# A three-layer graph network on one core: node blocks and places in the prologue, own rows and own products at other points in layers 1 and 2

## The chip, the core and the metric

The kernel runs on one core of a Trainium2 chip. A core has a matrix engine (PE, TensorE), a vector engine (DVE), a scalar engine with an activation table (ACT), a general engine (POOL, GpSimd) and an engine that here does nothing but start DMA transfers (SP, SyncE). Each engine takes its own instructions in the order in which they stand in the program, and waits at an instruction until what it needs is there. DMA transfers run beside the engines; they too are started in the order of the queue that they stand in. The metric is the time of one launch in microseconds of the device, the median of several runs.

## The reference

There are 6250 nodes with 256 features each and 100000 edges (src to dst), sorted by dst. Two GATv2 attention layers (4 heads of 64, with a loop edge at each node), the input added and normalized, then one GAT layer (8 heads of 32), added and normalized again:

```python
def _gatv2_layer(x, src, dst, n, Wl, Wr, att, b):
    xl = (x @ Wl).reshape(n, H, C)
    xr = (x @ Wr).reshape(n, H, C)
    e = jax.nn.leaky_relu(xl[src] + xr[dst], NEG_SLOPE)
    logits = jnp.einsum('ehc,hc->eh', e, att)
    m = jax.ops.segment_max(logits, dst, num_segments=n)
    ex = jnp.exp(logits - m[dst])
    denom = jax.ops.segment_sum(ex, dst, num_segments=n)
    alpha = ex / (denom[dst] + 1e-16)
    msg = xl[src] * alpha[:, :, None]
    out = jax.ops.segment_sum(msg, dst, num_segments=n)
    return out.reshape(n, H * C) + b
...
    h = _gatv2_layer(x, src, dst, n, Wl1, Wr1, att1, b1)
    h = jax.nn.elu(h)
    h = _gatv2_layer(h, src, dst, n, Wl2, Wr2, att2, b2)
...
x = _layernorm(x + _L0_gnn_ref(...), axis=-1)
x = _layernorm(x + _L1_gnn_ref(x, W, a, src, dst), axis=-1)
```

In the third layer Wh = x W per head, the logit of an edge is leaky_relu(s1[src] + s2[dst]) with s1 and s2 two projections of Wh, and the output is the softmax-weighted sum of Wh[src].

## The kernel before

**Blocks by degree.** The nodes are sorted by falling number of incoming edges into 49 blocks of 128, one node to a partition. Block b has a fixed number of neighbour slots, cols[b], from 27 in block 0 down to 9 in block 48. A row of a table for one slot of 128 nodes is fetched by one indirect DMA that POOL issues (`gather_rows`, L1300). In layers 1 and 2 there is one slot more, slot 0, for the node's own row (the loop edge).

**Prologue** (`make_plan`). From dst it finds each node's edges: the ends of the runs in 128 pieces of 784 edges by max and match_replace, eight at a time, 64 at most (L953, L955); counts by one-hot products (L981 to L986); the beginning of each list (begin_i), on which POOL fetches the pieces of the lists (piece_of, L1016, 17 gathers); each node's place in the order of degrees (place_f, place); then from to_hi, given and to_lo (L1088) the inverse, node_i, by 49 products on PE. moved (L1113 to L1123) and fill (L1133, L1140) bring the lists into their final form, and POOL stores them in near_d (L1143, six stores). `wrong`, `bad` and `fits` check that the plan holds; otherwise a general path is taken.

In between, table 1 is made: xl1 = x Wl1 with four more columns, 260 in all, in 49 blocks of 128 consecutive nodes. `load_x` loads x in seven parts of seven blocks on SP, `keep_x` stores the parts beside the lists in near_d, `turn` transposes a block (PE, then ACT's copy), `table` multiplies it and stores its 130 KB on SP (L860). `tables(n)` does n blocks; the calls are spread by hand over the prologue, in the order in which engines are to take them: 12, 1, 1, 1, 1, 12, 8, 4, and 9 more. The last column of table 1, a node's place, is written by a DMA of its own on ACT's queue, one number to a row (L1064). Two loads of W and a of layer 3 and the biases stand at the end of SP's prologue.

**Layers 1 and 2** (`layer2(0, ...)` and `layer2(1, ...)`). One loop over the 49 blocks, with the order of the instructions written out by hand. The iteration of block b issues, in this order: the loads of block b+3 (`start`), the gathers of block b+1 (`gather`), what block b+1 needs of its own (`ready`, which calls `own`: xr in PSUM, named pr, and a function that puts the own row into slot 0 of the first gathered tile), then `attend(b)`: DVE's max (z, L1571 or L1591), product (L1594) and sum (L1595) per tile of up to nine slots, the copy of the own row of b+1, the softmax weights (ACT exponentials, L1446), the first z of block b+1 (`first_z`, L1571), then `finish(b-1)`, the shares (L1451, L1452), ACT's copy by of some weights (L1473), the weighting (DVE at L1483, ACT at L1482), the sum over slots on PE (acc, L1490), and last the part of `finish(b-1)` that makes the rows of the next layer and stores them.

In layer 1, `own1` transposes the block's x (L1420, L1422) and multiplies it by Wl (pl) and Wr (pr); pl is copied into slot 0 by ACT (L1684). `finish1` makes two rows of layer 2's tables (pm, ACT L1704), stored by SP (L1708, L1709). In layer 2, `start2` loads the own rows of both tables into `two` three blocks ahead (SP, L1717, L1718); `own2` has ACT copy one half to pr (L1724) and the other into slot 0 (L1725). `finish2` normalizes, makes the row of layer 3's table (ACT L1738) and stores it (SP, L1740).

**Between layers.** `follow` stands in the iteration of block 47: the first 14, 12 and 11 gathers of the next layer's blocks 0, 1 and 2 (`EARLY`) read only rows of blocks 0 to 44 (`LATE = 4`), the lists having been sorted for that; the others read all rows. The gathered tiles are a ring of nine (`rowp`). Layer 3 has the same blocks without slot 0 and is summed on DVE.

Of the kernel before, what the change touches and what calls it, by code (L numbers as in the profile page):

```python
# [714 lines left out]
def make_plan(  # L715
# [39 lines left out]
    rowp = ctx.enter_context(tc.tile_pool(name="table1_row", bufs=10))  # L755
# [62 lines left out]
    def rows(i):  # L818
        return min(P, N - i * P)

    xs, turned, at = {}, {}, [0]

    def blocks(j):
        return j * PART, min((j + 1) * PART, N // P)

    def load_x(j):
        b0, b1 = blocks(j)
        xs[j] = work.tile([P, PART, F], F32, name="xt")
        nc.sync.dma_start(
            xs[j][:, : b1 - b0, :], x[b0 * P : b1 * P, :].rearrange("(c p) f -> p c f", p=P)  # L830
        )

    def keep_x(j):
        b0, b1 = blocks(j)
        nc.sync.dma_start(
            near_d[b0 * P : b1 * P, CM:].rearrange("(c p) f -> p c f", p=P), xs[j][:, : b1 - b0, :]
        )

    def turn(i):
        j, k = divmod(i, PART)  # L840
        if k == 0 and 2 <= j + 2 < NB // PART:
            load_x(j + 2)
        if k == 2:
            keep_x(j)
        xt = xs[j][:, k, :] if rows(i) == P else x_end
        pt = pst.tile([P, 2, P], F32, name="pt")
        for c in range(2):
            nc.tensor.transpose(pt[:, c, :], xt[:, c * P : (c + 1) * P], ident)
        turned[i] = work.tile([P, 2, P], F32, name="xT")
        nc.scalar.copy(turned[i], pt)  # L850

    def table(i):
        xT = turned.pop(i)
        w = wc[0].rearrange("p j c h d -> p j c (h d)")
        pm = pst.tile([P, W2], F32, name="pm")
        for c in range(2):
            nc.tensor.matmul(pm, xT[:, c, :], w[:, 0, c, :], start=c == 0, stop=c == 1)
        xl = rowp.tile([P, W2], F32, name="xl")
        nc.scalar.copy(xl, pm)
        nc.sync.dma_start(xl1_d[i * P : (i + 1) * P, :W2], xl)  # L860
# [24 lines left out]
    if rest:  # L885
# [19 lines left out]
    x_end = filled_tile("x_end", [P, F], 0.0)  # L905
# [13 lines left out]
    each_hi = iota("each_hi", [P, NB, NB], [[0, NB], [1, NB]], dtype=BF16)  # L919
    each_lo = iota("each_lo", [P, NB, P], [[0, NB], [1, P]], dtype=BF16)  # L920
    vals = one.tile([P, 3, NB], BF16, name="vals")
    nc.gpsimd.iota(vals[:, 0, :], pattern=[[0, NB]], base=0, channel_multiplier=1,
                   allow_small_or_imprecise_dtypes=True)
    nc.gpsimd.iota(vals[:, 1, :], pattern=[[1, NB]], base=0, channel_multiplier=0,
# [12 lines left out]
    edge = one.tile([P, RUNS + 1], F32, name="edge")  # L937
    nc.vector.memset(edge[:, :1], float(KE))
# [6 lines left out]
    )  # L945
    runs = one.tile([P, KE], F32, name="runs")
# [5 lines left out]
    for r in range(0, RUNS, 8):  # L952
        nc.vector.max(ends[:, r : r + 8], runs)  # L953
        if r + 8 < RUNS:
            nc.vector.match_replace(runs, ends[:, r : r + 8], runs, 0.0)  # L955
    tables(12)
    load(0, "r")
    for what in "lar":
        load(1, what)
    run_i = one.tile([P, RUNS], I32, name="run_i")  # L960
# [11 lines left out]
    nc.vector.tensor_copy(edge[:, 1:], part[:, 2, :])  # L972
    size = one.tile([P, RUNS], BF16, name="size")
    nc.vector.tensor_sub(size, edge[:, :RUNS], edge[:, 1:])
# [83 lines left out]
    nc.vector.tensor_scalar(vals[:, 2, :], count, 255.0, None, op0=OP.min)  # L1058
# [4 lines left out]
    with nc.allow_non_contiguous_dma(reason="one number to a row"):  # L1063
        nc.scalar.dma_start(  # L1064
            xl1_d[:NP, W2:].rearrange("(p b) w -> p b w", b=NB), place_f.unsqueeze(2)
        )
    nc.sync.dma_start(x_end[: rows(NB - 1)], x[(NB - 1) * P :, :])
    nc.sync.dma_start(near_d[(NB - 1) * P :, CM:], x_end)
# [5 lines left out]

    tables(12)


    to_hi = one.tile([P, NB, NB], BF16, name="to_hi")
    nc.vector.tensor_tensor(
        to_hi, each_hi, to[:, 1, :].unsqueeze(2).to_broadcast([P, NB, NB]), op=OP.is_equal  # L1080
    )
    given = one.tile([P, NB, 3, NB], BF16, name="given")
    for j in range(3):
        nc.vector.tensor_mul(
            given[:, :, j, :], to_hi, vals[:, j, :].unsqueeze(2).to_broadcast([P, NB, NB])
        )
    to_lo = one.tile([P, NB, P], BF16, name="to_lo")
    nc.vector.tensor_tensor(  # L1088
        to_lo, each_lo, to[:, 0, :].unsqueeze(2).to_broadcast([P, NB, P]), op=OP.is_equal
    )  # L1090
    pp = ps.tile([P, 3, NB], F32, name="pp")
    for b in range(NB):
        nc.tensor.matmul(pp, to_lo[:, b, :], given[:, b], start=b == 0, stop=b == NB - 1)
    tables(8)
# [12 lines left out]

    moved = one.tile([P, SEGS, STEP, WIDE], I32, name="moved")
# [39 lines left out]
    for k in spans:  # L1148
        lacking(*k)
        fill(*k)  # L1150
    tables(4)
    got = one.tile([P, 3, NB], F32, name="got")
    nc.vector.tensor_copy(got, pp)
    nc.vector.scalar_tensor_tensor(
        node_i, got[:, 0, :], float(NB), got[:, 1, :], op0=OP.mult, op1=OP.add
    )

    wrong = one.tile([P, KE + 2 * NB + 1], F32, name="wrong")  # L1160
    nc.vector.tensor_tensor(wrong[:, : KE - 1], dst_e[:, : KE - 1], dst_e[:, 1:], op=OP.is_gt)
    nc.vector.tensor_tensor(wrong[:, KE - 1 : KE], dst_e[:, KE - 1 :], next_e, op=OP.is_gt)
    nc.vector.tensor_tensor(wrong[:, KE : KE + NB], got[:, 2, :], most, op=OP.is_gt)
    nc.vector.tensor_tensor(
        wrong[:, KE + NB : KE + 2 * NB], off.rearrange("p s j -> p (s j)")[:, :NB],
        off_i.rearrange("p s j -> p (s j)")[:, :NB], op=OP.not_equal,
    )
    nc.vector.tensor_mul(
        wrong[:, KE + NB : KE + 2 * NB], wrong[:, KE + NB : KE + 2 * NB], count
    )  # L1170
    nc.vector.tensor_scalar(
        wrong[:, KE + 2 * NB :], base[:, :1], float(E), None, op0=OP.not_equal
    )
    bad = one.tile([P, 2], F32, name="bad")
    nc.vector.reduce_sum(bad[:, :1], wrong, axis=AX.X)
    nc.vector.tensor_scalar(
        bad[:, 1:], got[:, 2, :1], -float(held), 0.0, op0=OP.add, op1=OP.max
    )
    tables(NB)
    pb = ps.tile([P, 2], F32, name="pb", tag="ph")  # L1180
    nc.tensor.matmul(pb, ones, bad, start=True, stop=True)
    right(0)
    left(1, nc.vector)
    right(1)
    many = one.tile([P, 1], F32, name="many")
    nc.vector.tensor_scalar(many, pb[:, 1:], float(P), None, op0=OP.is_gt)
    nc.vector.tensor_add(many, many, pb[:, :1])
    nc.vector.tensor_scalar(fits, many, 0.0, None, op0=OP.is_equal)
    for c in range(2):
        nc.sync.dma_start(  # L1190
            wh[:, c, :F].rearrange("p (h d) -> p h d", h=H1),
            w3[:, c * P : (c + 1) * P, :].rearrange("h p d -> p h d"),
        )
    tables(7)
    for k, b in enumerate(biases):
        nc.sync.dma_start(
            fixed[:, k, :], bass.AP(tensor=b.tensor, offset=b.offset, ap=[[0, P], [1, F]])
        )
    for k, h in enumerate((a3[:, :D1], a3[:, D1:])):
        nc.sync.dma_start(  # L1200
            fixed[:, 2 + k, :].rearrange("p (h d) -> p h d", h=H1),
            bass.AP(tensor=h.tensor, offset=h.offset, ap=[[0, P], [2 * D1, H1], [1, D1]]),
        )
# [4 lines left out]
def tile_by_degree(  # L1208
# [62 lines left out]
    nc.sync.dma_start(wh_d[NP:], nobody[:, 1, :A1])  # L1271

# [263 lines left out]
    def layer2(i, table, of, width, start, own, finish, follow):  # L1536
# [5 lines left out]
        with ExitStack() as es:  # L1542
# [19 lines left out]
            def ready(b):  # L1562
                pr, put = own(work, ps, pst, b, state[b][0][0][:, 0, :W2])
                state[b].append(pr)
                later.append(put)
# [58 lines left out]
            for b in range(3):  # L1624
                if (i, b) not in loaded:
# [3 lines left out]
            gather(0)  # L1629
            ready(0)  # L1630
            later.pop()()
# [3 lines left out]
            for b in range(NB):  # L1635
# [27 lines left out]
                if b == 0:  # L1663
                    nc.tensor.matmul(acc, edges_of, few, start=False, stop=True)
                if last:
# [11 lines left out]

    def own1(work, ps, pst, b, row):
        xT = transposed(work, pst, x1[:, b, :])
        pl = pst.tile([P, W2], F32, name="pl", tag="tp")  # L1680
        product(pl, xT, wc[0][:, 0])
        pr = ps.tile([P, W2], F32, name="pr")
        product(pr, xT, wc[0][:, 1])
# [31 lines left out]
    def start2(b):  # L1715
        two = twop.tile([P, 2, W2], F32, name="two")
        nc.sync.dma_start(two[:, 0, :], xl2_d[b * P : (b + 1) * P])  # L1717
        nc.sync.dma_start(two[:, 1, :], xr2_d[b * P : (b + 1) * P])  # L1718
        kept[b] = two

    def own2(work, ps, pst, b, row):
        two = kept.pop(b)
        pr = ps.tile([P, W2], F32, name="pr")
        nc.scalar.copy(pr, two[:, 1, :])  # L1724
        return pr, lambda: nc.scalar.copy(row, two[:, 0, :])  # L1725
# [20 lines left out]
    kept, loaded = {}, set()  # L1746

    def begin2():
        begin(1, xl2_d, W2)
        for b in range(3):  # L1750
            start2(b)
            loaded.add((1, b))

    layer2(0, xl1_d[:, :], sources, W2 + 1, start1, own1, finish1, begin2)
# [118 lines left out]
```

## Time and profile before

| what | value |
|---|---|
| median of 3 runs | 3332.04 us (3331.96 to 3335.03) |
| the profiled execution's own time | 3328.12 us |
| its span | 3326.3 us |
| granted TensorE clock, mean | 0.711 |
| DVE, POOL, PE, ACT busy, share of the span | 83%, 73%, 43%, 33% |
| bytes moved by DMA | 395.84 MB, 119 GB/s |
| first gather of layer 1, of layer 2, of layer 3 | 131.25, 1211.98, 2235.97 us |

A group of the page gives line, engine, operation, written and read tiles and the count; then busy time and the mean of one in ns; then the idle time of the engine just before, and what ended most of it. In the timeline each line has start, length, engine, line, operation, and in brackets how long the engine stood before it and who released it; SPq is SP's queue, and "issue" is time for which the profile shows no wait. A stretch gives for each engine busy time and count, then the granted clock, the DMA engines' mean busy share and GB/s.

### The profile page before, as it was taken

Reading aid. Unit: us, or ns where it says so; the run is one execution under the profiler, and the core shown is the slowest. Engines: PE = TensorE matmul, PEld = TensorE weight load, DVE = VectorE, ACT = ScalarE, POOL = GpSimd, SP = SyncE. Lnnn points to the kernel's source line nnn. Section 1 sums busy time; section 2 is a strip of 40 time slices with the busy share of each in tenths; the row PEclk is TensorE's granted clock in tenths of the full one; section 3 lists DMA queues with packets and bytes.
Section 4 is the critical chain, followed back from the end, with each engine's and each line's share of the span. In section 5 each row is a group of like instructions: output and inputs, shape, how many; then the busy total and the mean of one; then the engine's idle time right before and its main releaser. Section 6 shows DMA issues by size and latency. Waiting matters only on the chain.

```text
span 3326.3 us, 24261 instructions
## 1 busy us (share of the span) xinstructions
PE 1416.2 (43%) x5423; PEld 1131.0 (34%) x5424; DVE 2755.3 (83%) x2527; ACT 1108.0 (33%) x4428; POOL 2435.2 (73%) x2588
## 2 busy tenths in 40 slices
PE   7346666666677773565656666662000000000000
PEld 5235554555555552454545454552000000000000
DVE  7599998889888888999999999985966767666766
ACT  3134434444444442444445666561000000000000
POOL 5477777777777767777777777767777777777776
PEclk8678888888888886777877878886555555555555
DMA  8744444444444444444444444444333333333333
GB/s 198 145 111 118 117 118 121 118 120 122 121 121 121 124 111 112 122 121 127 121 127 126 132 126 132 131 111 115 108 107 107 108 108 107 108 107 107 107 107 86
DMA packets 189103, 395.84 MB, mean 119 GB/s; under 512 B 56249, under 2 KB 107963, under 8 KB 188934
## 3 DMA queue, kind: packets, MB, share of 16 engines
q0 software_dynamic: 121392, 339.19, 39.0%
q1 hardware_dynamic: 59858, 53.27, 5.7%
q10 hardware_dynamic: 7700, 1.74, 0.5%
q8 instruction: 47, 0.77, 0.1%
q14 instruction: 106, 0.87, 0.1%
HBM read 354.02 MB, written 40.42 MB: 119 GB/s over the span
## 4 chain that ended last, share of the span: by engine, by line
POOL 23%; DVE 15%; issue 13%; PE 7%; DMA 3%; ACT 1%; DVEq 0%; POOLq 0%; ACTq 0%
POOL g L1300 22%; PE acc L1490 6%; DVE g L1483 3%; DVE z L1594 3%; DVE lg L1595 3%; DVE z L1571 3%; DVE z L1591 2%; DMA g<-xl_d,near_r 1%; POOL out L1812 1%; DMA out<-y,node_i 1%; PE pm L1427 1%; DVE stats L1522 0%; DMA g<-whs_d,near_r 0%; ACT sd L1526 0%; DVE weighted L1503 0%
## 5 line engine op out<-in xcount | busy, mean ns | idle before, releaser
L1300 POOL DMA_INDIRECT g<-xl_d,near_r x1569 | 1484.4, 946 | 485.8 <-issue 434.8
L1490 PE MATMUL acc<-g,ident 128*128 128x256 f32 x3408 | 972.0, 455 | 654.2 <-DVE g L1483 357.6
L1490 PEld LDWEIGHTS acc<-g,ident 128*128 128x128 f32 x3408 | 788.8, 235 | 838.3 <-DVE g L1483 378.4
L1300 POOL DMA_INDIRECT g<-whs_d,near_r x766 | 727.1, 949 | 233.3 <-issue 227.2
L1482 ACT ACTIVATE g<-g,by 128x64 f32<-128x64 f32 x2308 | 561.0, 336 | 1.6
L1595 DVE TENSOR_REDUCE lg<-z 128x28 f32<-128x1820 f32 (+4 forms) x234 | 497.4, 2125 | 8.1
L1594 DVE TENSOR_TENSOR z<-z,at 128x1820 f32<-128x1820 f32 (+4 forms) x234 | 496.9, 2124 | 4.7
L1483 DVE TENSOR_TENSOR g<-g,wt 128x1792 f32<-128x1792 f32 (+8 forms) x234 | 331.8, 1435 | 31.9 <-ACT by L1473 31.9
L1512 DVE TENSOR_REDUCE acc_v<-weighted 128x256 f32<-128x4096 f32 (+15 forms) x49 | 343.7, 7014 | 1.6
L1591 DVE TENSOR_TENSOR z<-g,pr 128x1820 f32<-128x1820 f32 (+3 forms) x138 | 299.6, 2171 | 23.2 <-DMA g<-xl_d,near_r 14.8
L1456 ACT ACTIVATE wt<-lg 128x128 f32<-128x128 f32 (+17 forms) x49 | 14.0, 285 | 803.6 <-DVE lg L1455 803.6
L1782 DVE TENSOR_TENSOR lg<-g,s_r 128x56 f32<-128x56 f32 (+4 forms) x111 | 22.4, 214 | 268.5 <-DMA g<-whs_d,near_r 212.2
L1571 DVE TENSOR_TENSOR z<-g,pr 128x2080 f32<-128x2080 f32 (+4 forms) x96 | 197.9, 2061 | 44.5 <-DMA g<-xl_d,near_r 13.5
L1503 DVE TENSOR_TENSOR weighted<-g,wt 128x1792 f32<-128x1792 f32 (+4 forms) x111 | 226.6, 2057 | 0.1
L1422 ACT COPY xT<-pt 128x256 f32<-128x256 f32 x147 | 55.0, 374 | 505.8 <-PE pt L1420 505.8
L1446 ACT ACTIVATE wt<-lg,top 128x19 f32<-128x19 f32 (+14 forms) x392 | 115.7, 295 | 234.2 <-DVE top L1439 224.7
L1427 PE MATMUL pm<-wcat,xT 128*128 128x260 f32 x392 | 99.0, 395 | 22.6 <-ACT xT L1422 22.6
L1427 PEld LDWEIGHTS pm<-wcat,xT 128*128 128x128 f32 x392 | 70.4, 189 | 42.8 <-ACT xT L1422 34.3
L1446 ACT ACTIVATION_READ_ACCUMULATOR wt<-lg,top 128x1 f32 x392 | 73.5, 187 | 0.0
L1812 POOL DMA_INDIRECT out<-y,node_i x49 | 50.1, 1022 | 25.8 <-issue 14.2
L1427 PE MATMUL pm<-wh_cat,xT 128*128 128x272 f32 x196 | 59.0, 424 | 22.6 <-ACT xT L1422 22.6
L1427 PE MATMUL pl<-wcat,xT 128*128 128x260 f32 x196 | 57.2, 415 | 25.2 <-ACT xT L1422 25.2
(250 smaller groups left out, 1527.3 us busy)
## 6 DMA issues: line engine op xcount, KB each, us to landing
g<-xl_d,near_r POOLq DMA_INDIRECT x1569, 2.8
g<-whs_d,near_r POOLq DMA_INDIRECT x766, 2.8
whs_d<-row SPq DMA_DIRECT2D x49, 132.0 KB, 2.0
xl_d<-xl SPq DMA_DIRECT2D x49, 130.0 KB, 7.9
xl_d<-row SPq DMA_DIRECT2D x49, 130.0 KB, 2.6
xr_d<-row SPq DMA_DIRECT2D x49, 130.0 KB, 2.9
two<-xl_d SPq DMA_DIRECT2D x49, 130.0 KB, 2.9
two<-xr_d SPq DMA_DIRECT2D x49, 130.0 KB, 3.3
```

The source lines that it names most:

```text
L1300: nc.gpsimd.indirect_dma_start(out=g[:, j + own - s0, :width], out_offset=None, in_=table, in_offset=source(of, b, j),)
L1427: nc.tensor.matmul(pm, xT[:, c, :], w[:, c, :], start=c == 0, stop=c == 1)
L1446: nc.scalar.activation(wt[:, :, h], lg[:, :S, h], AF.Exp, bias=top[:, h : h + 1], accum_out=den[:, h : h + 1],)
L1482: nc.scalar.mul(g4[:, t, h, :], g4[:, t, h, :], by[:, t - m, h : h + 1])
L1483: nc.vector.tensor_mul(g4[:, :m], g4[:, :m], wt[:, s0 : s0 + m, :].unsqueeze(3).to_broadcast([P, m, H, F // H]),)
L1490: nc.tensor.matmul(acc, ident, g4[:, t], start=False, stop=s0 + t == S - 1 and not more)
L1503: nc.vector.tensor_mul(prod[:, s0 - base : s1 - base, :].rearrange("p t (h d) -> p t h d", h=H), g[:, :n, :F].rearrange("p t (h d) -> p t ...
L1512: nc.vector.reduce_sum(part, prod[:, : s1 - base, :].rearrange("p s f -> p f s"), axis=AX.X)
L1571: nc.vector.tensor_max(z, rows[0][:, :n, :W2], xr[:, None, :].to_broadcast([P, n, W2]))
L1591: nc.vector.tensor_max(z, g[:, :n, :W2], xr[:, None, :].to_broadcast([P, n, W2]))
L1594: nc.vector.tensor_mul(z, z, at[:, None, :].to_broadcast([P, n, W2]))
L1595: nc.vector.reduce_sum(lg[:, s0:s1, :], z.rearrange("p t (h d) -> p t h d", h=H2), axis=AX.X)
```

## The change

It has four parts.

In the **prologue**, a block of table 1 is no longer 128 consecutive nodes but the nodes p·49 + b, p being the partition, which is how places and counts are laid out. x comes in parts of seven such blocks (one run of 7168 bytes per partition), and table 1 goes out seven blocks at a time with the place as its last column (`put_rows`), once the places are known; the DMA of single numbers is gone. The last partitions hold no node in some blocks: POOL zeroes them in the four last parts before they are loaded.

The run ends are found in two halves of each piece, 32 each. The inverse of the places is made from one-hots in groups of 16 blocks. The check and the node numbers stand ahead of moved and fill. The biases are loaded on ACT's queue, W and a of layer 3 by SP after the prologue. The calls of tables are 9, 1, 1, 1, 1, 1, 1, 1, 8 and 25.

In **layer 1**, x's transposition and the product pr of block b+2 are issued in the iteration of block b, after the sum and before the rows of `finish1`; `own1` has only pl left.

In **layer 2**, `two` holds only the row of xr. The own row is loaded by SP directly into slot 0, from `own2`, and ACT's copy is gone.

```diff
-    rowp = ctx.enter_context(tc.tile_pool(name="table1_row", bufs=10))
+    rowp = ctx.enter_context(tc.tile_pool(name="table1_row", bufs=4))
...
     def load_x(j):
-        b0, b1 = blocks(j)
+        b0, b1 = j * PART, (j + 1) * PART
         xs[j] = work.tile([P, PART, F], F32, name="xt")
-        nc.sync.dma_start(
-            xs[j][:, : b1 - b0, :], x[b0 * P : b1 * P, :].rearrange("(c p) f -> p c f", p=P)
-        )
+        if b1 <= odd:
+            nc.sync.dma_start(
+                xs[j],
+                bass.AP(tensor=x.tensor, offset=x.offset + b0 * F,
+                        ap=[[NB * F, P], [F, PART], [1, F]]),
+            )
+            return
+        k = max(odd - b0, 0)
+        nc.gpsimd.memset(xs[j][P - 32 :, k:, :], 0.0)
+        for p0, p1 in ((0, whole // 16 * 16), (whole // 16 * 16, whole)):
+            nc.sync.dma_start(
+                xs[j][p0:p1],
+                x[p0 * NB : p1 * NB, :].rearrange("(p b) f -> p b f", b=NB)[:, b0:b1, :],
+            )
...
+    def put_rows(j):
+        b0, b1 = j * PART, (j + 1) * PART
+        rows = made.pop(j)
+        nc.scalar.copy(rows[:, :, W2], placed[0][:, b0:b1])
+        nc.sync.dma_start(of_nodes(xl1_d[:NP], b0, b1), rows)
+
     def table(i):
...
-        xl = rowp.tile([P, W2], F32, name="xl")
-        nc.scalar.copy(xl, pm)
-        nc.sync.dma_start(xl1_d[i * P : (i + 1) * P, :W2], xl)
+        if k == 0:
+            made[j] = rowp.tile([P, PART, W2 + 1], F32, name="xl")
+        nc.scalar.copy(made[j][:, k, :W2], pm)
+        if k + 1 == PART and placed:
+            put_rows(j)
...
-    for r in range(0, RUNS, 8):
-        nc.vector.max(ends[:, r : r + 8], runs)
-        if r + 8 < RUNS:
-            nc.vector.match_replace(runs, ends[:, r : r + 8], runs, 0.0)
-    tables(12)
+    for h, part_runs in enumerate((runs[:, HALF:], runs[:, :HALF])):
+        for r in range(h * HR, (h + 1) * HR, 8):
+            nc.vector.max(ends[:, r : r + 8], part_runs)
+            if r + 8 < (h + 1) * HR:
+                nc.vector.match_replace(part_runs, ends[:, r : r + 8], part_runs, 0.0)
+    tables(9)
...
-    with nc.allow_non_contiguous_dma(reason="one number to a row"):
-        nc.scalar.dma_start(
-            xl1_d[:NP, W2:].rearrange("(p b) w -> p b w", b=NB), place_f.unsqueeze(2)
-        )
...
+    placed.append(place_f)
+    for j in sorted(made):
+        if (j + 1) * PART <= at[0]:
+            put_rows(j)
...
+    for b0 in range(0, NB, T):
+        n = min(T, NB - b0)
+        s = slice(b0, b0 + n)
+        oh_hi = hot.tile([P, NB, T], BF16, name="oh_hi")[:, :, :n]
...
+        if b0 + n < NB:
+            tables(1)
...
-    tables(NB)
+    tables(8)
...
-    def layer2(i, table, of, width, start, own, finish, follow):
+    def layer2(i, table, of, width, start, ahead, own, finish, follow):
...
+            for b in range(2):
+                ahead(work, ps, pst, b)
             ready(0)
...
+                if b + 2 < NB:
+                    ahead(work, ps, pst, b + 2)
                 if last:
                     last[0]()
...
+    def ahead1(work, ps, pst, b):
+        xT = transposed(work, pst, x1[:, b, :])
+        pr = ps.tile([P, W2], F32, name="pr")
+        product(pr, xT, wc[0][:, 1])
+        kept[b] = xT, pr
+
     def own1(work, ps, pst, b, row):
-        xT = transposed(work, pst, x1[:, b, :])
+        xT, pr = kept.pop(b)
         pl = pst.tile([P, W2], F32, name="pl", tag="tp")
         product(pl, xT, wc[0][:, 0])
-        pr = ps.tile([P, W2], F32, name="pr")
-        product(pr, xT, wc[0][:, 1])
         return pr, lambda: nc.scalar.copy(row, pl)
...
     def start2(b):
-        two = twop.tile([P, 2, W2], F32, name="two")
-        nc.sync.dma_start(two[:, 0, :], xl2_d[b * P : (b + 1) * P])
-        nc.sync.dma_start(two[:, 1, :], xr2_d[b * P : (b + 1) * P])
-        kept[b] = two
+        two = twop.tile([P, W2], F32, name="two")
+        nc.sync.dma_start(two, xr2_d[b * P : (b + 1) * P])
+        loaded[b] = two
...
     def own2(work, ps, pst, b, row):
-        two = kept.pop(b)
+        nc.sync.dma_start(row, xl2_d[b * P : (b + 1) * P])
         pr = ps.tile([P, W2], F32, name="pr")
-        nc.scalar.copy(pr, two[:, 1, :])
-        return pr, lambda: nc.scalar.copy(row, two[:, 0, :])
+        nc.scalar.copy(pr, loaded.pop(b))
+        return pr, None
```

The code of moved, fill and the check is unchanged and only stands in another order.

## The prediction

> **What bounds the kernel now.** I read the page's groups first, then the time by stretches, then POOL's waits at the two borders between layers, then the timeline of one block in each loop. All working is against the profiled execution, 3328.1 us with a span of 3326.3; the median shown is 3332.0, so 3.9 us is added at the end.
>
> ```profile
> L1300 POOL DMA_INDIRECT g<-xl_d,near_r x1569 | 1484.4, 946 | 485.8 <-issue 434.8
> L1300 POOL DMA_INDIRECT g<-whs_d,near_r x766 | 727.1, 949 | 233.3 <-issue 227.2
> ```
>
> One gather is 0.95 us busy and 0.30 us of issue: 1.25 us, 2335 times, 2919 us of the 3326. POOL is the bound wherever it has something to gather.
>
> ```profile
> 0.00:131.00 131.00, 76.26 (x418) 61.88 (x419) 89.74 (x137) 39.83 (x136) 56.50 (x78) 0.83 0.94 190
> 131.00:700.00 569.00, 340.09 (x1317) 273.55 (x1317) 506.50 (x441) 225.95 (x921) 430.48 (x455) 0.80 0.44 117
> 1690.00:2236.00 546.00, 344.64 (x1238) 274.08 (x1238) 513.31 (x429) 322.99 (x1342) 402.82 (x427) 0.80 0.47 126
> 2282.00:3326.00 1044.00, 2.68 (x6) 1.50 (x6) 730.59 (x772) 68.00 (x197) 778.49 (x819) 0.50 0.39 106
> ```
>
> The columns after the length are PE, PEld, DVE, ACT and POOL busy. POOL has 74 to 76 of every 100 us in all three layers, which is 0.95 of 1.25, back to back. But DVE has 94% in layer 2's second half (513 of 546), so the loop behind POOL has hardly any slack. It matters at a border: the next layer's gathers need rows that the loop has stored.
>
> ```profile
> 2235.97 0.95 POOL L1300 DMA_INDIRECT g<-whs_d,soon  x1 [13.48 <-DVE stats L1522]
> ```
>
> POOL ends layer 2's gathers at 2222.5 and waits 13.5 us. The early gathers of layer 3 (37, 46 us) read blocks 0 to 44 only; block 44's row is issued by SP at 2233.26, after the sum of block 45, and 2.7 us later POOL starts. At the border before, POOL waits 16.87 us at 1211.98 in the same way. So each border stands where block 46 of the DVE and PE loop puts it, and what a loop loses per block arrives in full; layer 3, POOL-bound, can't win it back.
>
> The loop of layer 2, block 36 to 37:
>
> ```profile
> 2051.75 0.38 ACT L1738 COPY row<-pm 128x264 f32<-128x264 f32 x1 [1.27 <-PE pm L1427]
> 2052.08 0.40 ACT L1724 COPY pr<-two 128x260 f32<-128x260 f32 x1
> 2052.15 0.32 SPq L1740 DMA_DIRECT2D whs_d<-row  x1
> 2052.39 0.42 ACT L1725 COPY g<-two 128x260 f32<-128x260 f32 x1
> 2052.52 0.43 SPq L1717 DMA_DIRECT2D two<-xl_d  x1
> 2052.84 2.05 DVE L1571 TENSOR_TENSOR z<-g,pr 128x1820 f32<-128x1820 f32 x1 [1.02 <-ACT g L1725]
> 2052.99 0.46 SPq L1718 DMA_DIRECT2D two<-xr_d  x1
> ```
>
> The previous sum (L1490) ends at 2049.85; call that A. Then come a transposition, ACT's copy, the product, ACT's row, pr and own row, and z starts at A+2.99. Over all blocks read so: in blocks 1 to 18 DVE's own work ends last (z at A+6.0 to 9.6, no idle); in 19 to 48 z comes at A+3.0 to 3.9, most of them at 3.00 exactly with DVE idle 0.3 to 2.0 us. There this chain is the bound.
>
> **Layer 2's own row.** ACT's 0.42 us copy goes. In its place SP loads the row of block b+1 straight into slot 0, and DVE's z (L1571) waits for the landing. The load used to be issued three blocks ahead. Now it is issued in the iteration that uses it, and SP works in order: ahead of it stand the store whs_d<-row of the previous iteration, which waits for ACT's row, and two<-xr. So whatever SP's idle time, the load can't go before A+2.30 (the store, 2052.15). The xr load takes the place of xl's at A+2.67, the row's load follows 0.45 later at A+3.12.
>
> ```profile
> two<-xl_d SPq DMA_DIRECT2D x29, 130.0 KB, 2.9
> two<-xr_d SPq DMA_DIRECT2D x29, 130.0 KB, 3.2
> ```
>
> Landing, median, in this stretch: the load that stands second takes 3.2 us, and this one will stand second. A+3.12+3.2 = A+6.3, with 0.1 to DVE's start A+6.4, against 3.0: a loss of 3.4 us in a block where the chain rules. Bounds: the fastest tenth of xl's loads is 2.4 us (A+5.6), the slowest 4.1 (A+7.3). I walked blocks 1 to 48, each z taking the later of DVE's own end and A plus the delay, the rest of the block kept: at block 46 the loss is 67 us by 5.6, **89 us by 6.4**, 117 by 7.3 (28 blocks by 3.4 is 95; some have DVE's end in between). Behind z on DVE stand the statistics, the shares, the weighting (L1483) and so the sum and the next A: nothing of the chain goes on meanwhile. The gathers wait later for free tiles, which costs nothing extra, since the loop then sets the end.
>
> The Trainium skill ("DMA: Bandwidth & Descriptors", section "Anatomy of one DMA") fits a transfer by about 2.0 us fixed plus bytes over 436e3 per us; that is on another queue than SP's and by estimate 2.3 us for 130 KB, faster than the 2.9 and 3.2 of this trace. With it z would stand at A+5.5 and the loss at 64 us. The same page's "Rules for kernel authors" says to issue a transfer early and wait on it late; the change does the opposite with this one.
>
> **Layer 1's products.** After A the order was transposition of h, two products pm, transposition of x, pl, pr. Now x's transposition and pr of block b+2 come first, then h, pm twice, and pl of block b+1 next iteration. The work is the same; the last of it is pl in place of pr.
>
> ```profile
> 1196.27 1.04 PE L1427 MATMUL pr<-wcat,xT 128*128 128x260 f32 x4
> 1196.47 0.38 ACT L1684 COPY g<-pl 128x260 f32<-128x260 f32 x1 [1.23 <-PE pl L1427]
> 1197.38 0.06 DVE L1671 MEMSET pr<- 128x4 f32 x1 [3.87 <-PE pr L1427]
> 1197.62 1.51 DVE L1571 TENSOR_TENSOR z<-g,pr 128x1300 f32<-128x1300 f32 x1 [0.17 <-ACT wt L1446]
> 1199.56 0.16 ACT L1473 COPY by<-wt 128x16 f32<-128x16 f32 x1
> ```
>
> A is 1191.85. The last product ended at A+5.46 and z began at A+5.77, after a 0.06 us memset. Then: product, ACT's copy of 0.38, z, some 0.1 later. The copy is worth more on ACT: it moves from A+4.6 to A+5.4, and the four exponentials, the casts, three activations and by (L1473) follow it, 0.78 us later. DVE's weighting waits for by. What ACT has free ahead of by is 0.70 us in blocks 21 to 31, 0.43 in 32 to 40, 0.2 in 41 to 45, nothing in 46 to 48: 11 × 0.08 + 9 × 0.35 + 5 × 0.58 + 3 × 0.78 = 9.3. I take **+9**. Bounds: −3, if PE's order saves the wait for ACT between transposition and product and all else hides; +22, if 0.78 counts in every block from 21 on.
>
> **The prologue.** DVE's part gets shorter: the eight max and seven replace passes (0.98, 0.09, 0.96 us over 784 columns) run over halves, now 8 and 6 of half the length: 16.6 us of span becomes about 9.9 with the fixed part of each pass kept, 6.7 less. The place's one-hots (2.66 + 7.80 + 6.69 = 17.2 us) become four groups; by the 0.56 and 1.22 us of the groups at L981 and L986 about 10.8. POOL's 17 piece gathers took 40.3 to 72.9, with 2.3 to 6.3 us for some beside those long DVE passes; they gain too. The node numbers and the checks (104.4 to 108) move ahead of moved.
>
> ```profile
> 78.02 0.81 DVE L1113 COPY moved<-piece_of 128x1173 int32<-128x1173 int32 x1 [8.17 <-DMA piece_of<-list_d,begin_i]
> 100.28 5.83 POOL L1143 DMA_DIRECT2D near_d<-moved  x6 [27.41 <-DVE moved L1140]
> 124.61 0.24 POOL L1247 IOTA numbers<- 128x128 f32 x1 [18.50 <-DMA xl_d<-xl]
> 131.25 0.95 POOL L1300 DMA_INDIRECT g<-xl_d,near_r  x1 [2.23 <-issue]
> ```
>
> moved starts near 68 instead of 78, the near lists are issued by about 97. But the last wait is not theirs: POOL stood 18.5 us at the border for xl_d<-xl, and the 16 DMA engines are 0.94 busy over the prologue. What the change takes off them: place_f's 6272 four-byte writes (15.7 us to landing on a queue of its own) and x_end. What it moves: the W and a loads of layer 3 to after the border. What it adds in waits: the last part of x is loaded by SP behind POOL's memset of its tail rows (0.75 us for a like one, L879), and POOL does that behind the near lists, so at 97 to 99. SP's x part 6 then has to land (6.7 us for 896 KB), be turned and multiplied in seven blocks, and be stored, once as rows (now 7 blocks in one store; 896 KB took 10.0), so 122 to 128, beside some 4.6 MB of other stores. Then 6.6 us to the first gather, as now. That is about 131: I take **0**, from −10 (DVE's gain arrives whole: lists at 97, landed at 112, gather at 120) to +9 (the last store at 133).
>
> **Sum.** 3328.1 + 0 + 9 + 89 = 3426; with 3.9 for the median **3430**. The ends of the terms don't fall together: lowest 3332 − 10 − 3 + 67 = 3386, highest 3332 + 9 + 22 + 117 = 3480.
>
> **The rivals.** *The load is hidden* (small change). If SP issued it ahead of the store, or z did not wait for it, z would stand at A+2.6 (pr's end), and the walk gives −6 at block 46: 3332 + 9 − 6 = 3335. For it: SP idles most of a block, and the slot is free long before. Against it: one queue in order, and the store waits for a row that is made after A.
>
> *The prologue decides* (faster). If the row is in time and the first gather follows DVE's chain, −11 is carried through all layers by the back-to-back gathers: 3332 − 11 − 6 + 0 = 3315. It decides as soon as x's last part lands by 105, so that stores end before the lists. For it: DVE's 13 us are real, and 8.17 us of waiting goes as well. Against it: the memset's place behind the lists, and the DMA engines at 0.94.
>
> *The load costs half.* Should the store and the row's load overlap so that z is at A+4 or 4.5, the walk gives 20 to 45 us, 3360 to 3390.
>
> **How the numbers follow.** The forecast's case has 0.84, the hidden load 0.05, the prologue 0.08, the half price 0.03. The forecast's own range, 3386 to 3480, has about 0.94 of its case; taking in the half price, 3360 to 3480 holds 0.82. This measurement can tell 0.2% (6.7 us) from no change. Slower: 0.84 + 0.03 = 0.87. Same: most of the hidden load, 0.04. Faster: the prologue and the rest, 0.09.
>
> **What would show it.** In layer 2 the z at L1571's place waits for the DMA of its own row in blocks 19 to 48, at A+5.6 to 7.3, and DVE's busy share in that stretch falls from 94% to about 81 (513 of 635). POOL's first gather of layer 3 starts near 2334. In layer 1 the border moves by about 9, DVE waiting for by. The first gather stays near 131 and its last wait is a store or load behind part 6 of x. It is wrong if z does not wait there, or if the first gather comes before 121.

## The result, and the profile after

The changed kernel takes 3459.32 us (median of 4 runs, 3456.72 to 3463.17); the kernel before, on the same chip, 3333.53. The ratio is 1.0378, 95% interval 1.036 to 1.0396: slower by 126 us. Forecast was 3430 us, 98 us over the 3332.04 that it started from.

Where it went, with the layers marked off by POOL's first gather of each (profiled executions, spans 3326.3 and 3458.8 us; that of the kernel before was 5 us faster than its median, so the stretches add up to more than 126):

| stretch | before | after | difference |
|---|---|---|---|
| start to first gather of layer 1 | 131.25 | 145.00 | +13.8 |
| layer 1, to first gather of layer 2 | 1080.73 | 1093.13 | +12.4 |
| layer 2, to first gather of layer 3 | 1023.99 | 1122.77 | +98.8 |
| layer 3, to its last gather | 1066.50 | 1073.32 | +6.8 |

The sum is 131.8, and the spans differ by 132.5. Three quarters are in layer 2. First its loop, at the block that the prediction showed (the timeline of the changed kernel, blocks 36 to 37, without POOL):

```profile
2136.42 0.38 PE L1446 MATMUL pt<-ident,near_r 128*128 128x128 f32 x2
...
2138.48 0.38 ACT L1776 COPY row<-pm 128x264 f32<-128x264 f32 x1 [1.27 <-PE pm L1453]
...
2138.82 0.40 ACT L1762 COPY pr<-two 128x260 f32<-128x260 f32 x1
2138.89 0.32 SPq L1778 DMA_DIRECT2D whs_d<-row  x1
2139.26 0.47 SPq L1753 DMA_DIRECT2D two<-xr_d  x1
2139.61 0.26 DVE L1465 TENSOR_REDUCE top<-lg 128x4 f32<-128x60 f32 x1
...
2140.10 0.32 SPq L1760 DMA_DIRECT2D g<-xl_d  x1
...
2143.10 2.05 DVE L1598 TENSOR_TENSOR z<-g,pr 128x1820 f32<-128x1820 f32 x1 [3.23 <-DMA g<-xl_d]
```

The sum of the block before (the A of the prediction) ends at 2136.6. pr is there at 2139.22 and DVE is free at 2139.87, but z starts at 2143.10: the row's load (L1760) left SP at 2140.10 only, behind the store (L1778), which had waited for ACT's row, and behind two's load. Over blocks 19 to 48 the load leaves at A+3.51 in the mean, z follows it by 3.15, so that z stands at A+6.66, and DVE idles 3.94 us a block, 118 us in all. Its group in layer 2 of the changed kernel (1690 to 2366 us; busy, mean, then idle time ahead and what ended it):

```profile
L1598 DVE TENSOR_TENSOR z<-g,pr 128x2080 f32<-128x2080 f32 (+4 forms) x32 | 67.5, 2109 | 114.3 <-DMA g<-xl_d,near_r 73.0 <-DMA g<-xl_d 40.8 <-ACT wt L1472 0.5
```

and the same group of the kernel before (1690 to 2236):

```profile
L1571 DVE TENSOR_TENSOR z<-g,pr 128x2080 f32<-128x2080 f32 (+4 forms) x31 | 65.7, 2120 | 15.2 <-ACT g L1725 8.5 <-DMA g<-xl_d,near_r 5.7
```

The same work, and over seven times the idle time ahead of it. A reader could take "DMA g<-xl_d,near_r" for a late neighbour gather; but the gathers of that tile had all been issued some 54 us before (block 36's by 2089.3). The tile has two writers, and the one that lands at the moment of z's start is the row.

The prologue of the changed kernel, from the timeline of each engine, first DVE's:

```profile
67.53 0.31 DVE L1141 COPY got<-pp 128x147 f32<-128x147 f32 x1 [6.39 <-PE pp L1124]
...
77.70 0.16 DVE L1174 TENSOR_SCALAR many<-pb 128x1 f32<-128x1 f32 x1 [3.55 <-PE pb L1169]
...
78.46 0.81 DVE L1182 COPY moved<-piece_of 128x1173 int32<-128x1173 int32 x1 [0.22 <-issue]
```

POOL's, which stores the lists, then clears the tail of the last part of x, and at the end waits for that part's copy beside the lists:

```profile
100.83 5.83 POOL L1212 DMA_DIRECT2D near_d<-moved  x6 [26.83 <-DVE moved L1209]
106.66 1.62 POOL L833 MEMSET xt<- 32x1792 f32 x1
...
139.76 1.04 POOL L1706 DMA_INDIRECT near_r<-near_d,node_i  x1 [4.16 <-DMA near_d<-xt]
```

SP's, with the load of that part:

```profile
108.31 0.85 SPq L835 DMA_DIRECT2D xt<-in_x  x2
```

PE's, which goes on when it has landed:

```profile
123.53 0.66 PE L860 MATMUL pt<-ident,xt 128*128 128x128 f32 x2 [25.12 <-DMA xt<-in_x]
```

And two stretches; the columns end in PE clock, DMA share and GB/s:

```profile
90.00:100.00 10.00, 8.41 (x46) 6.81 (x44) 9.86 (x6) 5.34 (x18) 0.00 (x0) 1.00 0.01 2
115.00:120.00 5.00, 0.00 (x0) 0.00 (x0) 0.00 (x0) 0.00 (x0) 0.00 (x0) 0.50 1.02 98
```

DVE was ready for moved at 61 (the last of its bits ended there), but the node numbers and the check, now ahead, wait for PE (the 6.39 and 3.55 above), and moved starts at 78.46, half a microsecond later than before the change. So the lists are stored at 100.83 to 106.66, the memset of x's last part comes after them, and the load of that part is issued at 108.31, when the DMA engines are full with the near lists' pieces of 152 bytes. It takes 15 us to land; PE stands 25. The last block's rows and the part's copy follow, and the first gather comes 5 us after the copy has landed. From 90 to 100 the DMA engines had moved next to nothing (0.01).

Layer 1, block 46 of the changed kernel, where the sum before ended at 1213.43; the timeline, of ACT and DVE:

```profile
1218.87 0.38 ACT L1720 COPY g<-pl 128x260 f32<-128x260 f32 x1 [0.50 <-PE pl L1453]
...
1219.28 1.51 DVE L1598 TENSOR_TENSOR z<-g,pr 128x1300 f32<-128x1300 f32 x1 [2.81 <-ACT g L1720]
```

and DVE's weighting:

```profile
1222.15 1.75 DVE L1509 TENSOR_TENSOR g<-g,wt 128x1536 f32<-128x1536 f32 x1 [0.83 <-ACT by L1499]
```

z stands at A+5.85 against the 5.77 of the kernel before, but the weighting at A+8.72 against 7.91.

### The profile page after: what moved, and what is told of

It reads as the page before. It is cut to its first block, busy times and chain, and to the rows that moved or that the text cites. A ratio compares the mean times of both kernels' runs of the same rounds, so it can differ in the third digit from the quotient of the medians.

```text
span 3458.8 us, 24465 instructions
## 1 busy us (share of the span) xinstructions
PE 1429.4 (41%) x5423; PEld 1138.5 (33%) x5424; DVE 2744.6 (79%) x2542; ACT 1095.7 (32%) x4386; POOL 2428.7 (70%) x2589
## 5 line engine op out<-in xcount | busy, mean ns | idle before, releaser
L1598 DVE TENSOR_TENSOR z<-g,pr 128x2080 f32<-128x2080 f32 (+4 forms) x96 | 197.9, 2061 | 208.5 <-DMA g<-xl_d,near_r 84.3
L1552 ACT ACTIVATE sd<-mv,eps 128x1 f32<-128x1 f32 x98 | 28.9, 294 | 215.4 <-DVE mv L1550 215.4
L1849 POOL DMA_INDIRECT out<-y,node_i x49 | 50.2, 1025 | 26.0 <-issue 14.2
```

The source lines that it names most:

```text
L1598: nc.vector.tensor_max(z, rows[0][:, :n, :W2], xr[:, None, :].to_broadcast([P, n, W2]))
```

## The experiments

All are edits of the changed kernel. The first four ran on a chip where the kernel before takes 3327.2 us (3324.99 to 3329.28, 7 runs), so ratios are compared, not times. The times expected were worked out for the chip of the result; by the ratios the four come to 3356, 3361, 3447 and 3448 us there, each inside its expected range.

**Layer 2's row by ACT, as before.** `start2` loads both rows again; in `own2`:

```diff
-        nc.sync.dma_start(row, xl2_d[b * P : (b + 1) * P])
         pr = ps.tile([P, W2], F32, name="pr")
-        nc.scalar.copy(pr, loaded.pop(b))
-        return pr, None
+        nc.scalar.copy(pr, two[:, 1, :])
+        return pr, lambda: nc.scalar.copy(row, two[:, 0, :])
```

> The changed kernel with layer 2's own row as before the change: both rows loaded three blocks ahead, ACT copies one of them into slot 0. Theory (z waits for a row that is loaded one block ahead): z in blocks 19 to 48 back at 3.0 us after the sum, the stretch from the first gather of layer 2 to that of layer 3 back from 1123 to about 1024 us, the time about 3357 us (3350 to 3366). Rival (layer 2 is longer because of something else in the change, such as what layer 1 leaves behind or the buffers): less than 20 us gained, over 3440.

3349.01 us, ratio 1.0067 (1.005 to 1.0084). Layer 2 takes 1021.8 us between first gathers, as before the change (1024.0). The whole loss of layer 2 goes with this one part; the rival is out.

**The store on ACT's queue.**

```diff
-                nc.sync.dma_start(wh_d[b * P : (b + 1) * P], row)
+                nc.scalar.dma_start(wh_d[b * P : (b + 1) * P], row)
```

> The changed kernel with layer 2's store of layer 3's row started by ACT instead of SP, so that the load of the own row has no store ahead of it on SP's queue; it is still loaded one block ahead. Theory (the place on SP's queue behind a store that waits for ACT's row): the row lands in time, z in blocks 19 to 48 at 2.6 to 3.0 us after the sum, layer 2 99 to 105 us shorter, about 3355 us (3345 to 3370). Rival (one block ahead is too late for a transfer of 2.9 us whatever stands ahead of it, or the gathers' traffic slows it): z still over 5 us after the sum, 3440 to 3465.

(The profile calls wh_d whs_d.) 3354.98 us, ratio 1.0083 (1.0066 to 1.01); layer 2 1025.4 us, 97 us shorter (99 to 105 expected), and z at A+3.09 in most of blocks 19 to 48 (2.6 to 3.0 expected). The row is still loaded one block ahead, by the same transfer beside the same gathers (3.0 us to landing in the median), and z waits for ACT again, not for the row. So it was the place in SP's queue, behind a store that waits, and not the transfer. But the gain over before, which ACT's missing copy should have brought, isn't there either. Timeline of this kernel, ACT's and DVE's lines at block 45:

```profile
2223.45 0.17 ACT L1777 COPY s_r<-pm 128x8 f32<-128x8 f32 x1
2223.58 0.33 ACTq L1778 DMA_DIRECT2D whs_d<-row  x1
2223.95 0.38 ACT L1762 COPY pr<-two 128x260 f32<-128x260 f32 x1 [0.33 <-issue]
...
2224.36 1.78 DVE L1598 TENSOR_TENSOR z<-g,pr 128x1560 f32<-128x1560 f32 x1 [0.83 <-ACT pr L1762]
```

Starting the store holds ACT for 0.33 us just ahead of pr; the copy that is gone took 0.42.

The Trainium skill ("DMA: Bandwidth & Descriptors", section "Issuing engines are not separate DMA queues") says that starting transfers on several engines saves only the time to start them, usually small beside the transfer. Here the choice of the starting engine moved the kernel by 3%, since one engine's starts also wait for one another.

**Layer 1's products as before.** `ahead1` does nothing, and `own1` has both again:

```diff
-        xT, pr = kept.pop(b)
+        xT = transposed(work, pst, x1[:, b, :])
         pl = pst.tile([P, W2], F32, name="pl", tag="tp")
         product(pl, xT, wc[0][:, 0])
+        pr = ps.tile([P, W2], F32, name="pr")
+        product(pr, xT, wc[0][:, 1])
```

> The changed kernel with layer 1's own row as before the change: transposition and both products of block b+1 after the rows of the next layer. Theory (ACT's own-row copy and all that stands behind it come later): the stretch from the first gather of layer 1 to that of layer 2 falls by about 12 us to 1081, the time to about 3447 (3442 to 3452). Rival (the border moves because of the later first gather and the traffic at the start, not the order of products): within 4 us of 3459.

3440.48 us, ratio 1.034 (1.0323 to 1.0358). Layer 1 is 1080.7 us between first gathers, as before the change: 12.4 us come from the order of the products.

**The remaining blocks of table 1 ahead of the lists.**

```diff
+    tables(NB)
     for k in spans:
         lacking(*k)
         fill(*k)
-    tables(NB)
```

> The changed kernel with the remaining blocks of table 1 written ahead of the filling of the lists, so that POOL clears the last part of x before it stores the near lists, not after. Theory (SP's load of the last part of x stands behind a memset that stands behind six stores): the load goes out near 85 us instead of 108, table 1 is complete near 112, the first gather near 128 instead of 145, the time 3440 (3436 to 3449). Rival (the stores of the near lists, 152 bytes each, hold the DMA engines until 122 whatever the order): first gather at 138 or later, over 3450.

3443.84 us, ratio 1.0344 (1.0327 to 1.0361). The memset now runs at 85.81, the load goes out at 87.42, and the first gather comes at 130.59 (expected near 128), 9 us ahead of the 139.3 to 140.1 of the three runs above on this chip. What is left is named in POOL's waits to 150 us of this kernel:

```profile
POOL numbers L1263 <- DMA near_d<-moved: 17.9, 1, 17.9
```

Now the near lists, stored at 101.8 to 107.6, are last.

The other runs fell on two chips where every kernel takes over 3830 us: the first try of each of the next four on one (the kernel before 3872, 3838 to 3896 over 31 runs), the second tries and the last experiment on the other (3870, 3838 to 3887 over 27 runs). Engines there stand for several us with no releaser that the profile names; the same code of layer 1 took 1313 and 1305 us in two runs of one kernel, and 1296 and 1313 in two of another. So stretches of the loops can't be compared there to under 20 us; the ratios, over 6 to 10 runs, the prologue and the places inside a block can.

**The prologue alone** (both edits of layers undone), twice:

> The change's prologue alone: layers 1 and 2 as before the change. Theory (the last part of x, behind the memset, sets the first gather at 139 to 145): ratio to the kernel before 1.003 (1.0015 to 1.0045), 8 to 14 us, all of it ahead of the first gather; layer 1 at 1081 us and layer 2 at 1022 to 1024 between first gathers. Rival (the parts act on one another, so that layers 1 and 2 stay longer by what the prologue leaves, such as wh and a loaded late): over 1.006.

> The change's prologue alone once more, since on the chip of the first try the gathers were slower throughout and hid differences of this size. Theory: 8 to 14 us behind the kernel before, all ahead of the first gather, which comes at 139 to 145; layer 1 between first gathers 1081, layer 2 1022 to 1025. Rival (the prologue also lengthens layers 1 and 2): layer 1 over 1084 or layer 2 over 1028.

Ratios 0.9999 (0.9956 to 1.0042) and 1.0044 (1.0013 to 1.0075), first gather at 144.45 and 145.65. The place of the loss agrees: the prologue of the kernel before, in the last experiment (the loops alone, on the chip of the second run), has its first gather at 135.79, 9.9 us earlier, inside the expected 8 to 14. The ratios don't settle the size better than this, and what was expected of layers 1 and 2 can't be read there. Nor were the gathers slower throughout, as the second expectation supposes: those of layers 1 and 2 took 0.95 us as before, those of layer 3 1.04 against 0.95.

**Lists ahead of checks**, on top of it: moved, the remaining blocks of table 1 and fill stand before got, as moved and fill did before the change.

```diff
+    moved = one.tile([P, SEGS, STEP, WIDE], I32, name="moved")
...
+    tables(NB)
+    for k in spans:
+        lacking(*k)
+        fill(*k)
     got = one.tile([P, 3, NB], F32, name="got")
...
-    tables(8)
...
-    tables(NB)
```

> The prologue alone again, with the lists filled ahead of the node numbers and checks, as before the change, and the remaining blocks of table 1 written ahead of the filling. Theory (DVE waits 15 us for PE at the node numbers and the check's sum; POOL's memset is late): moved starts near 61 us instead of 78, near lists issued by 94, first gather near 120 (115 to 126), ratio to the kernel before 0.9965 (0.995 to 0.998). Rival (the near lists' and the tables' stores together are bound by the DMA engines): first gather no earlier than 130, ratio 1.000 or more.

Ratio 0.9964 (0.9926 to 1.0001). The near lists were stored from 86.96, 14 us earlier, and had landed at 112.7. But the first gather came at 130.80, not near 120: there the rival was right. The ratio is the one that the theory named, with an interval that just reaches the rival's 1.000. POOL's lines:

```profile
112.67 0.24 POOL L1262 IOTA numbers<- 128x128 f32 x1 [19.88 <-DMA near_d<-moved]
...
125.77 1.04 POOL L1705 DMA_INDIRECT near_r<-near_d,node_i  x1 [12.62 <-DMA near_d<-xt]
```

Now the copies of x are last, and the DMA engines are 1.06 to 1.09 busy from 95 to 125. The end of the prologue is DMA traffic, and of the 14 us that DVE saves most don't arrive; against the 135.79 of the kernel before's prologue (on the other of these two chips) it is 5.

**Layer 2's row ahead of the store**: besides, the store of the iteration before is written after the row's load, and ACT makes pr two blocks ahead. Twice:

```diff
                 if b + 1 < NB:
                     ready(b + 1)
+                put_kept()
                 rows, cut, wt, new = attend(b)
```

> That prologue and layer 1 as before; in layer 2 the own row comes by SP as in the change, but on SP's queue ahead of the store of the iteration before, and ACT makes pr two blocks ahead. Theory (z then waits for nothing that is made after the sum; DVE's own work is the bound): z in blocks 19 to 48 with no idle time on DVE, layer 2 between first gathers 8 to 14 us under e6's, to 1010 to 1015. Rival (the transfer or ACT gives it back elsewhere, as a store started by ACT did): within 4 us of e6's layer 2.

> Layer 1 as before, the rest as in the kernel with all mended. Theory: layer 1 1081, layer 2 1010 to 1015, so that the two transpositions alone are worth 10 us between this and the one ahead of it. Rival (layer 1's gain is only a later or earlier border): no difference over 4 us in the time.

Ratios 0.9997 (0.9964 to 1.003) and 1.0009 (0.9979 to 1.0038): level with the kernel before. Layer 2 took 1197.9 and 1189.5 us, against 1186 to 1195 for the three runs without the edit: no sign of the gain that was expected. The trace shows why, on these chips. Two groups of DVE in the first run, from 2061 us to the border at 2624:

```profile
L1597 DVE TENSOR_TENSOR z<-g,pr 128x2080 f32<-128x2080 f32 (+4 forms) x28 | 58.8, 2099 | 12.0 <-ACT pr L1763 7.8 <-remote 2.2 <-ACT g L1507 0.3
L1476 DVE RECIPROCAL den<-den 128x4 f32<-128x4 f32 x29 | 5.0, 172 | 55.1 <-ACT wt L1471 46.8 <-issue 8.3
```

z itself does what the theory says: it waits 12 us in all, where the kernel with lists ahead of checks has 85 in the like stretch. But DVE now stands 55 us further on, at the sum of the weights (den), for ACT's exponentials (57 in the second run), and 17 at the statistics, where it did not wait at all without the edit. That is the rival's case: ACT gives it back. Whether it would on a chip of the first kind was not tried.

**Two transpositions one after the other**: besides, layer 1 as in the change, but h's transposition directly behind x's, and pr behind both (`more` is the product that `ahead1` now returns). Twice:

```diff
             def last(more=None):
                 hT = transposed(work, pst, h)
+                if more:
+                    more()
```

> e7 with the change's layer 1, in which PE does the two transpositions one after the other, x's of block b+2 and then h's, then pr, pm twice and pl. Theory (in the change's order PE waits 0.46 us twice for ACT's copies, and pl ends the chain): pl and with it z and by come 0.8 us earlier per block than in the change; layer 1 between first gathers 1071 (1066 to 1077) against 1081 before and 1093 in the change. Rival (ACT's chain to by sets the pace, whatever PE's order): 1085 to 1093.

> The kernel with lists ahead of checks, layer 2's row ahead of the store and layer 1's two transpositions, once more on another chip. Theory: first gather near 131, layer 1 1071 (1066 to 1077), layer 2 1010 to 1015, in all 15 to 26 us ahead of the kernel before. Rival (ACT's chain to by in layer 1, and DVE's own work in layer 2, leave nothing to win): layer 1 1081 or more, layer 2 1021 or more.

Ratios 0.9929 (0.9896 to 0.9961) and 0.9946 (0.9924 to 0.9967): this one beats the kernel before on both of these chips, by 0.5 to 0.7%, where the changed kernel is 3.8% behind on the chip of the result. It differs from the one ahead only in layer 1, so that part is worth about that much there: 25 and 20 us between the medians, where 10 was expected. The place inside the block agrees with the theory: z of layer 1 stands at A+4.90 in both runs (median of blocks 19 to 48) against 5.85 in the changed kernel, 0.95 us earlier where 0.8 was expected, and the weighting at A+7.96 and 8.01 against 8.88. Why the time gains more than was expected is open. The 20 us that the second run is ahead of the kernel before lie in the forecast's 15 to 26; it wasn't run on a chip of the first kind.

**The loops alone**, with the prologue of the kernel before:

> The prologue of the kernel before, with the two loops of the kernel with all mended. Theory (the DMA engines, not the order of DVE's work, set the first gather, since the near lists and the tables have to be out by then in both): first gather at 131, within 3 us of the mended prologue's, the same time as that kernel's within 4 us. Rival (the mended prologue's shorter work on DVE is worth more): the mended prologue 5 us or more ahead.

Ratio 0.9964 (0.9938 to 0.999), first gather at 135.79 against 128.5 to 130.8 in the five runs with the mended prologue. The expectation missed on that point: the mended prologue is some 5 to 7 us ahead at the first gather, which the intervals of the ratios neither show nor exclude.

## Why the prediction was right, and where it wasn't

*Layer 2's own row* was right in mechanism, place and sign: z of blocks 19 to 48 waits for its own row, behind the store. Its size was 89 us and measured 98.8, by the two runs that take the wait away (1022 and 1025 against 1123) 97 to 101. DVE's share from block 17 to the border was forecast at 81% and is 80 (511 of 642). The term that was small is the load's issue: A+3.12 was forecast, A+3.51 measured, since SP's next start follows two's by 0.84 us in the block shown (0.79 in the median), not 0.45. The landing was about right (3.2 and 0.1 to DVE's start, against 3.15 from issue to z). The same walk with 6.7 in place of 6.4 gives 97 to 98. (Two readings were off without weight: the 2335 gathers leave out the 74 early ones, and block 19's z stood at A+5.0, not under 3.9.)

*Layer 1* was forecast at 9, measured 12.4 and confirmed by undoing it. Its copy and its ACT queue behaved as worked out: by comes about 0.1 us later in most of blocks 21 to 31, 0.3 to 0.4 in 32 to 40, 0.6 in 41 to 45, 0.82 from 46 on. But these delays don't add up as the forecast added them. Counted from the first gather, the sum of block 35 still ends only 0.3 us later than before. All else up to the 10.2 us by which the sum ahead of block 47's z (block 45's) ends later comes in the ten blocks from 36 on: 5.2 by the delays of by, and 4.7 by sums that PE takes longer over (8.86 us against 7.57 in block 41, 8.85 against 7.26 in block 43, 6.98 against 5.45 in block 45). The cause of these was not sought. What was left out is the row itself: with x's transposition and pr ahead of it, a row is stored at A+4.09 instead of A+2.26, and the border waits for block 44's row. With its 1.8 us, and 0.4 more from that store's start to the first gather (3.10 against 2.71), it is 12.4. So the place and the sign were right, and that 9 came as near as it did is in part luck.

*The prologue* was the step that failed: "moved starts near 68 instead of 78", so 0, with +9 as the outer bound, against 13.8. (In the first three experiments the first gathers came at 139.3 to 140.1, but on a chip from which there is no profile of the kernel before.) DVE's gain was real and was there at 61, and DVE's own work on the node numbers and the checks takes 7.2 us more: that gives the forecast's 68. What the forecast put at nothing is the wait for PE, which was at products and tables (6.4 and 3.6 us there, with 4.7 at the one-hots before). The memset then stood at 106.7, not at 97 to 99, and took 1.62 us, not 0.75; and the last part of x took 15 us, not 6.7, to land in the traffic of the near lists. The chain named, part 6 behind a memset behind six stores, was the right one: moving it alone brought back 9 us on one chip. The lower bound (−10, lists decide) is refuted by the run with the lists ahead of the checks: they were 14 us earlier, and the first gather was no earlier than 130.80. That the time still fell into the range is due to the width of layer 2's bounds, not to the prologue's.

*The rival "the load is hidden"* has its condition (issued ahead of the store) shown by the store on ACT's queue, though with 1025 and not with the 6 us that the walk gave: the start on ACT took its place. *The rival "the prologue decides"* fell already on the row and on DVE's waits for PE; with those waits away, the run with the lists ahead of the checks shows the DMA engines as the next limit, as the argument against the rival had it. That each border carries a loop's loss in full is shown by undoing the parts: with layer 2's undone the ratio falls from 1.0378 to 1.0067, 103 us, with layer 1's to 1.034, 13 us, about what each had lost in its own stretch (each ratio is good to 6 us). What came after the last border, 6.8 us, was not in the forecast: 4.6 of it is the first wait behind the early gathers (5.85 against 1.25 at the same gather), which read all rows and so wait for block 48's; the other 2.2 are not placed.

## What to carry to other kernels

A load that is moved to the iteration that uses it is late by what stands ahead of it in its engine's queue; here the same transfer of 3 us cost nothing once the waiting store was out of its way. Look for the instruction there that waits for something late, and for the sum that it hangs on. Work moved ahead on one engine takes its waits for other engines with it; list them before its time is called saved. When small stores and the last load of a chain come due together, as they did here at the end of the prologue, it counts which goes first: that alone was worth 9 us.

## What the runs showed of the hardware

Starting one 132 KB store cost ACT 0.33 us in its own sequence, nearly the 0.42 of the copy that it was to save.

In the changed kernel the DMA engines moved 98 GB/s at a busy share of 1.02 from 115 to 120 us, while lists in pieces of 152 bytes were stored and x's last part loaded; with table 1, the copies of x and the first of W, from 135 to 140 us, they moved 346 GB/s at 1.08.

On the two chips of the later runs layer 1 took 1281 to 1313 us instead of 1081 to 1093, with the same gathers of 0.95 us and 0.30 of issue. DVE, PE and ACT stood still together where the profile names no releaser, in the second run of the prologue alone from 594.5 to 598.5 us:

```profile
594.13 0.36 ACT L1727 ACTIVATE pos<-acc 128x256 f32<-128x256 f32 x1
598.48 0.06 DVE L1703 MEMSET pr<- 128x4 f32 x1 [7.25 <-remote]
```

What holds them was not tried.
